# Graph network of two layers: four more groups of each layer from products, and another order at the border of two batches

## The chip, the core and the metric

The kernel runs on one core of a Trainium2 chip. The metric is the device time of one execution in microseconds. Before the change the median of three runs is 3701.22 us (3698.91 to 3702.09).

## What is computed

12,500 nodes carry 48 features, and 200,000 edges are sorted by their target `dst`. Cut to what matters, the reference is:

```
# layer 0
tmp = concatenate([x[dst], x[src], edge_attr_32], axis=1)
msg = relu(tmp @ W1 + b1) @ W2 + b2
x1  = layernorm(x + segment_sum(msg, dst))
# layer 1
m   = relu(x1[src] + edge_attr_48)
out = layernorm(x1 + (1 + eps) * x1 + segment_sum(m, dst))
```

For an edge's message, the row `x[src]` has to be fetched from an arbitrary place in the table. The sums over `dst` are local, since the edges are sorted.

## The kernel before

**Groups and steps.** The edges are cut into 391 groups of 512 (four tiles of 128 edges). Each layer is one loop over steps `k` (`run`, L620): in each step every stage runs for its own group, as in `(sum1, 1)`, which handles group `k - 1`. Nothing reorders the instructions: each engine's queue holds them in the order in which the Python code makes them, and a wait holds up everything behind it on that engine.

**Two ways to the source rows.** Most groups fetch their 512 rows by four indirect gathers that POOL makes (`gather`, L246, shown as L247), six groups ahead (`AHEAD`), in layer 1 into a pool of twelve buffers (`xs_pool`, L165). The groups of `PE_GROUPS0` (layer 0: 65, 85, ..., 16 groups) and `PE_GROUPS` (layer 1: 20, 30, ..., 38 groups) need no gather: TensorE makes their rows as products of one-hot matrices with the whole table, which lies on chip in three bf16 pieces (`xp`, 98 blocks of 128 rows).

**A batch of products** (`products`, L530) makes two groups, that is eight tiles. `place` (L479) has DVE write eight one-hots of the row within a block (`which_e`, L485), and PE transposes them into a PSUM tile `which` (L490). In layer 1 ACT makes a copy of it in SBUF (L539). Then for each of the 98 blocks an engine selects those edges whose source lies in that block: DVE from `which` (L495), or ACT in two instructions from the copy (L500, L502). PE multiplies each selected one-hot with the block (`multiply`, L507; eight products a block) into three PSUM tiles `ps`. These are opened and closed by matmuls of zeros (`edge_of`, L515). At the end DVE adds the three pieces into `made` (`take`, L523). Blocks are multiplied one step after they were selected.

In layer 1 a batch takes 20 steps of five blocks (`BPS`), the third by ACT (`BY_ACT = 2`). Its PSUM tiles come from `banks = ("pm", "ph", "ph", "pm")` with two buffers to each name: `ps` takes two buffers of `ph` and one of `pm`, `which` the other of `pm`. In layer 0 a batch takes 40 steps with two and three blocks in turn (`BPS0`), all selected by DVE, with one buffer to each tile.

**Layer 1's own stages.** `fill1` (L693) makes the one-hots of targets on DVE (`hot`, L695), from a pool `late` of four buffers (L686), two steps ahead. `message1` (L702) adds rows and edge features on DVE (`m`, L705 for gathered rows, L709 for products), and ACT takes the relu (`msg`, L711). `sum1` (L717) sums the group by four f32 matmuls (L725, two records each), one step later. Twelve groups share a PSUM bank, opened and closed by zeros (L722, L730). `drain1` (L734) adds a closed bank to the table of sums, and where a segment of 896 nodes is complete, `finish1` (L456) transposes its sums (L394) and DVE and ACT normalize and store them. The stages stand in this order within a step:

```
[(fetch1, -AHEAD), (fill1, -2), (sum1, 1), (drain1, 4), (message1, 0), (some_products, -AHEAD)]
```

Between the layers `front` (L759) makes six groups' rows of the last segment by products while the gathers of the other segments already run.

**Layer 0** has its stages in L567 to L618: transposes of the assembled rows (`turn0`, L587), two matrix products (L598, L613), relu (L602), and the window sums on DVE (L387). In its last steps the finished segments are loaded again by SP and split into the three pieces (`lead0`, L640; `END0`).

Of the kernel before, what the change touches and what calls it, by code (L numbers as in the profile page):

```python
# [32 lines left out]
F32 = mybir.dt.float32  # L33
I32 = mybir.dt.int32
BF16 = mybir.dt.bfloat16
# [4 lines left out]
P = 128  # L40
Q = 128
N = 12500
E = 200000
D = 48
# [4 lines left out]
NT = -(-N // Q)  # L49
# [9 lines left out]
NSEG = NT // NB  # L59
# [4 lines left out]
AHEAD = 6  # L64
# [3 lines left out]
GB = 12  # L68
FRONT = 6
FIRST = 20  # L70
EVERY = 10
NPE = 38
BEGIN1 = 4
BATCH = 2
BPS = 5
BY_ACT = 2
PIECES = 3

FIRST0 = 65
EVERY0 = 20  # L80
NPE0 = 16
BPS0 = (2, 3)
SPLIT0 = 2
BEGIN0 = 20
END0 = 341

PE_GROUPS0 = [FIRST0 + EVERY0 * i for i in range(NPE0)]
PE_GROUPS = [FIRST + EVERY * i for i in range(NPE)]
assert FRONT % BATCH == 0 and NPE % BATCH == 0
assert PE_GROUPS[0] >= FRONT  # L90

assert PE_GROUPS[-1] < NCHUNK and PE_GROUPS0[-1] < NCHUNK
assert 2 * NT < BATCH * EVERY0 * sum(BPS0) and BEGIN0 > SPLIT0 + NSEG + 1
assert CHUNK * N % E == 0
assert NSEG * NB == NT
STEP = CHUNK * N // E
# [64 lines left out]
def windowed(ctx, tc, dram, flag, x, src, dst, e32, e48, w1, b1, w2, b2, eps, out):  # L161
# [15 lines left out]
    psum = layer0.enter_context(tc.tile_pool(name="psum0", bufs=1, space=bass.MemoryType.PSUM))  # L177
# [109 lines left out]
    for op, by, plus, to in (  # L287
# [3 lines left out]
        nc.vector.tensor_scalar(  # L291
            bits[:, FRONT : FRONT + NPE, :], src_g[:, FIRST : PE_GROUPS[-1] + 1 : EVERY, :],
            by, None, op0=op,
        )
        nc.vector.tensor_scalar(
            bits[:, FRONT + NPE :, :], src_g[:, FIRST0 : PE_GROUPS0[-1] + 1 : EVERY0, :],
            by, None, op0=op,
        )
        nc.vector.tensor_scalar(to, bits, plus, None, op0=ALU.add)
    begin.close()  # L300
    onehots = layer0.enter_context(tc.tile_pool(name="onehots0", bufs=2 * max(BPS0)))
    product = layer0.enter_context(tc.tile_pool(name="product0", bufs=1))
# [126 lines left out]
    def rows_of(table, s):  # L429
        return table[s * SN : (s + 1) * SN, :].rearrange("(t p) d -> p t d", p=Q)  # L430

    def split(t, s):
        for i in range(PIECES):
            piece = xp[:, s * NB : (s + 1) * NB, i, :]
            nc.scalar.activation(piece, t, AF.Copy)
            if i < PIECES - 1:
                rest = node.tile([Q, NB, D], F32, name="rest")
                nc.vector.tensor_tensor(rest, t, piece, op=ALU.subtract)
                t = rest

    def finish0(s):
# [6 lines left out]
        if s < NSEG - 1:  # L448
            nc.scalar.dma_start(rows_of(front_dram, s), x1)
        if last_group(s) >= END0:  # L450
            split(x1, s)
# [15 lines left out]
    def last_group(s):  # L467

        return max(g for g in range(NCHUNK) if low(g) < (s + 1) * SN)
# [7 lines left out]
    PER = 512 // (PIECES * D)  # L477

    def place(first, tiles, name, bufs):  # L479

        which = psum.tile([Q, tiles, P], BF16, name=name, bufs=bufs)
        which_e = product.tile([P, tiles, Q], BF16, name="which_e")
        for j in range(tiles):
            i = first + j // TPC
            nc.vector.tensor_scalar(  # L485
                which_e[:, j, :], iota_1, part[:, i, j % TPC : j % TPC + 1],
                block[:, i, j % TPC : j % TPC + 1], op0=ALU.is_equal, op1=ALU.mult,
            )
        for j in range(tiles):
            nc.tensor.transpose(which[:, j, :], which_e[:, j, :], ident16)  # L490
        return which

    def select(which, b):
        o = onehots.tile([Q, which.shape[1], P], BF16, name="o")
        nc.vector.tensor_scalar(o, which, float(b + 1), None, op0=ALU.is_equal)  # L495
        return o

    def select_by_act(copy, b):
        square = product.tile([Q, copy.shape[1], P], BF16, name="square")
        nc.scalar.activation(square, copy, AF.Square, bias=less[:, b : b + 1])  # L500
        o = onehots.tile([Q, copy.shape[1], P], BF16, name="o_act", bufs=2)
        nc.scalar.activation(o, square, AF.Relu, bias=1.0, scale=-1.0)  # L502
        return o

    def multiply(ps, o, b):
        for j in range(o.shape[1]):
            nc.tensor.matmul(  # L507
                ps[j // PER][:, j % PER, :], o[:, j, :], xp[:, b, :, :],
                start=False, stop=False, skip_group_check=True,
            )  # L510

    def edge_of(ps, start):
        for t in ps:
            n = t.shape[1] * PIECES * D
            nc.tensor.matmul(  # L515
                t.rearrange("p k c d -> p (k c d)"), zeros[:, :P], zeros[:, :n],
                start=start, stop=not start,
            )

    def take(ps, first, batch):  # L520
        xs = product.tile([P, batch * TPC, D], F32, name="made", bufs=FRONT // BATCH)
        for k, t in enumerate(ps):
            nc.vector.tensor_reduce(  # L523
                xs[:, k * PER : k * PER + t.shape[1], :], t.rearrange("p k c d -> p k d c"),
                AX.X, ALU.add,
            )
        for i in range(batch):
            made[ahead[first + i]] = xs[:, i * TPC : (i + 1) * TPC, :]

    def products(begin, count, batch, blocks, per_step, by_act, banks, bufs):  # L530


        tiles = batch * TPC
        for first in range(begin, begin + count, batch):
            which = place(first, tiles, banks[0], bufs)
            copy = None
            if by_act is not None:
                copy = product.tile([Q, tiles, P], BF16, name="copy", bufs=2)
                nc.scalar.activation(copy, which, AF.Copy)  # L539
            ps = [  # L540
                psum.tile([P, min(PER, tiles - k), PIECES, D], F32, name=banks[1 + k // PER],
                          bufs=bufs)
                for k in range(0, tiles, PER)
            ]
            edge_of(ps, True)
            last = []
            todo, step = list(blocks), 0
            while todo:
                n = per_step[step % len(per_step)]
                now = [  # L550
                    (b, select_by_act(copy, b) if i == by_act else select(which, b))
                    for i, b in enumerate(todo[:n])
                ]
                todo, step = todo[n:], step + 1
                for c, o in last:
                    multiply(ps, o, c)
                last = now
                yield
            for c, o in last:
                multiply(ps, o, c)  # L560
            edge_of(ps, False)
            take(ps, first, batch)


    cat, h, pt, ph, pa, hot = {}, {}, {}, {}, {}, {}
# [54 lines left out]
    def run(stages, adds, finish, lead):  # L620
# [13 lines left out]

    whole = {}
    work0 = products(
        FRONT + NPE, NPE0, BATCH, range(NT), BPS0, None, ("which", "sums0", "sums1", "sums2"), 1
    )

    def lead0(k):  # L640
# [10 lines left out]
        for s in range(NSEG):  # L651
# [3 lines left out]
            if k == SPLIT0 + s + 2:  # L655
                split(whole.pop(s), s)
            if last_group(s) < END0:
                if k == END0 + 2 * s + 1:
                    whole[s] = seg.tile([Q, NB, D], F32, name="whole", bufs=2)
                    nc.sync.dma_start(whole[s], rows_of(x1_dram, s))  # L660
                if k == END0 + 2 * s + 4:
                    split(whole.pop(s), s)
# [7 lines left out]
    def fetch1(g, table):  # L670
        cat[g] = xs_pool.tile([P, TPC, D], F32, name="xs")
        for j in range(TPC):
            gather(cat[g][:, j, :], table, g, j)
# [9 lines left out]


    layer0.close()
    late = ctx.enter_context(tc.tile_pool(name="late", bufs=4))  # L686
    psum = ctx.enter_context(tc.tile_pool(name="psum", bufs=1, space=bass.MemoryType.PSUM))
    onehots = ctx.enter_context(tc.tile_pool(name="onehots", bufs=8))
    product = ctx.enter_context(tc.tile_pool(name="product", bufs=1))
# [67 lines left out]
    banks = ("pm", "ph", "ph", "pm")  # L757

    def front():  # L759
# [18 lines left out]
            before = ps, first  # L778
        take(*before, BATCH)

    rest = products(FRONT, NPE, BATCH, range(NT), (BPS,), BY_ACT, banks, 2)

    def some_products(g):
        if g >= BEGIN1:
            next(rest, None)
# [3 lines left out]
    def lead1(k):  # L789
        for s in range(NSEG):  # L790
# [3 lines left out]
    front()  # L794
    run(
        [(lambda g: g >= FRONT and g not in PE_GROUPS and fetch1(g, x1_dram), -AHEAD), (fill1, -2),
         (sum1, 1), (drain1, 4), (message1, 0), (some_products, -AHEAD)],
        None, None, lead1,
    )

# [210 lines left out]
```

## Time and profile before

| | |
|---|---|
| median of three runs | 3701.22 us |
| the profiled execution | 3699.33 us |
| its span, first to last instruction | 3697.6 us |
| mean granted TensorE clock | 0.885 |
| busy PE, PEld | 91%, 80% |
| busy DVE, ACT, POOL | 73%, 37%, 75% |
| gathers on POOL, layer 0 | 1500, 953 ns each |
| gathers on POOL, layer 1 | 1388 and 24, 951 and 958 ns each |
| products of batches (weight loads of L507) | 21,336 |

PE is the matmul queue, PEld its weight loads[...]. A PE that is shown busy is not PE at its peak, because matmuls overlap and because the clock that is granted to it changes. So the share of busy time alone does not tell which engine sets the pace. Times in the timeline are microseconds from the start of the span. Layer 0 ends near 1915 us with its last segment, the products of `front` lie between 1922 and 1957 us, and layer 1 runs from there to the end.

### The profile page before, as it was taken

Reading aid. Unit: us, or ns where it says so; the run is one execution under the profiler, and the core shown is the slowest. Engines: PE = TensorE matmul, PEld = TensorE weight load, DVE = VectorE, ACT = ScalarE, POOL = GpSimd, SP = SyncE. Lnnn points to the kernel's source line nnn. Section 1 sums busy time; section 2 is a strip of 40 time slices with the busy share of each in tenths; the row PEclk is TensorE's granted clock in tenths of the full one; section 3 lists DMA queues with packets and bytes.
Section 4 is the critical chain, followed back from the end, with each engine's and each line's share of the span. In section 5 each row is a group of like instructions: output and inputs, shape, how many; then the busy total and the mean of one; then the engine's idle time right before and its main releaser. Section 6 shows DMA issues by size and latency. Waiting matters only on the chain. (4 is left out here: it accounts for less than half of the span.)

```text
span 3697.6 us, 87599 instructions
## 1 busy us (share of the span) xinstructions
PE 3348.4 (91%) x33806; PEld 2968.8 (80%) x33806; DVE 2683.3 (73%) x5415; ACT 1365.6 (37%) x2178; POOL 2774.8 (75%) x2923
## 2 busy tenths in 40 slices
PE   5888998998999899887889999999999999999996
PEld 4887988897888798886768887888888888888884
DVE  4765876676777686674438788788878888888883
ACT  2211211121112121113215555565556555655562
POOL 7777777777777777777776777777777777777776
PEclk8887988898989898897659999999999999999996
DMA  4222222122222212223211122122212221222121
GB/s 94 50 50 44 47 50 52 39 55 47 46 47 53 51 44 49 49 48 68 46 35 37 43 46 46 42 52 46 46 43 46 51 46 37 52 46 51 37 52 35
DMA packets 326421, 177.43 MB, mean 48 GB/s; under 512 B 144384, under 2 KB 325744, under 8 KB 326000
## 3 DMA queue, kind: packets, MB, share of 16 engines
q0 software_dynamic: 93184, 71.75, 11.3%
q1 hardware_dynamic: 203152, 88.86, 9.0%
q10 hardware_dynamic: 29664, 11.16, 1.1%
q8 instruction: 269, 4.41, 0.5%
q14 instruction: 152, 1.25, 0.1%
HBM read 156.51 MB, written 15.03 MB: 46 GB/s over the span
## 5 line engine op out<-in xcount | busy, mean ns | idle before, releaser
L247 POOL DMA_INDIRECT cat<-in_x_dram,src_i x1500 | 1429.2, 953 | 460.8 <-issue 310.3
L247 POOL DMA_INDIRECT xs<-x_dram,src_i x1388 | 1320.0, 951 | 435.9 <-issue 291.1
L507 PEld LDWEIGHTS <-o 128*128 128x128 bf16 x18296 | 1250.4, 102 | 99.4 <-DVE o L495 41.9
L495 DVE TENSOR_SCALAR o<-pm 128x1024 bf16<-128x1024 bf16 x1503 | 942.5, 686 | 62.2 <-ACT copy L539 27.1
L507 PE MATMUL ph<-xp,o 128*128 128x144 bf16 x8976 | 808.8, 231 | 0.0
L602 ACT ACTIVATE h<-ph 128x512 f32<-128x512 f32 x391 | 233.0, 596 | 1110.7 <-PE pa L613 1086.1
L598 PE MATMUL ph<-wcat,cat_t 128*128 128x128 f32 x3128 | 507.4, 313 | 106.4 <-ACT h L602 106.3
L598 PEld LDWEIGHTS ph<-wcat,cat_t 128*128 128x128 f32 x3128 | 448.0, 221 | 127.4 <-ACT h L602 120.8
L725 PE MATMUL pt<-hot,msg 128*48 128x128 f32 x3128 | 447.9, 290 | 56.5 <-ACT msg L711 56.5
L495 DVE TENSOR_SCALAR o<-which 128x1024 bf16<-128x1024 bf16 x784 | 495.3, 680 | 3.1 <-PE which L490 3.0
L507 PE MATMUL sums<-xp,o 128*128 128x144 bf16 x6272 | 488.6, 238 | 0.0
L725 PEld LDWEIGHTS pt<-hot,msg 128*48 128x48 f32 x3128 | 341.0, 129 | 141.4 <-ACT msg L711 63.8
L507 PE MATMUL pm<-xp,o 128*128 128x144 bf16 x2978 | 438.9, 230 | 0.0
L613 PE MATMUL pa<-cat,h 128*128 128x48 f32 x3128 | 431.6, 285 | 5.4 <-DVE pa L606 5.1
L613 PEld LDWEIGHTS pa<-cat,h 128*128 128x128 f32 x3128 | 429.2, 212 | 6.8 <-issue 4.7
L500 ACT ACTIVATE square<-copy,less 128x1024 bf16<-128x1024 bf16 x380 | 430.7, 1133 | 0.7
L502 ACT ACTIVATE o_act<-square 128x1024 bf16<-128x1024 bf16 x380 | 401.6, 1057 | 17.2 <-PE pm L507 5.8
L587 PE MATMUL pt<-ident,cat 128*128 128x128 f32 x1564 | 292.4, 302 | 82.5 <-DMA cat<-in_x_dram,src_i 79.3
L695 DVE TENSOR_TENSOR hot<-pa,rel 128x512 f32<-128x512 f32 x391 | 269.8, 690 | 97.6 <-PE pt L725 96.6
L591 DVE COPY cat_t<-pt 128x512 f32<-128x512 f32 x391 | 266.9, 683 | 72.3 <-PE pt L587 68.9
L711 ACT ACTIVATE msg<-m 128x192 f32<-128x192 f32 x391 | 141.5, 362 | 456.9 <-DVE m L705 408.4
L587 PEld LDWEIGHTS pt<-ident,cat 128*128 128x128 f32 x1564 | 214.7, 171 | 110.2 <-DMA cat<-in_x_dram,src_i 105.7
(118 smaller groups left out, 2412.1 us busy)
## 6 DMA issues: line engine op xcount, KB each, us to landing
e48c<-in_e_dram SPq DMA_DIRECT2D x78, 480.0 KB
e32c<-in_e_dram SPq DMA_DIRECT2D x78, 320.0 KB
cat<-in_x_dram,src_i POOLq DMA_INDIRECT x1500
xs<-x_dram,src_i POOLq DMA_INDIRECT x1388
wcat<-a SPq DMA_DIRECT2D x391, 24.0 KB
a<-a ACTq DMA_DIRECT2D x14, 256.0 KB
a<-a ACTq DMA_DIRECT2D x14, 192.0 KB
x_seg<-in_x_dram SPq DMA_DIRECT2D x14, 168.0 KB
```

Of the source, the lines that this page charges most:

```text
L247: nc.gpsimd.indirect_dma_start(out=t, out_offset=None, in_=table, in_offset=bass.IndirectOffsetOnAxis(ap=src_i[:, g * TPC + j : g * TPC + ...
L495: nc.vector.tensor_scalar(o, which, float(b + 1), None, op0=ALU.is_equal)
L500: nc.scalar.activation(square, copy, AF.Square, bias=less[:, b : b + 1])
L502: nc.scalar.activation(o, square, AF.Relu, bias=1.0, scale=-1.0)
L507: nc.tensor.matmul(ps[j // PER][:, j % PER, :], o[:, j, :], xp[:, b, :, :], start=False, stop=False, skip_group_check=True,)
L587: nc.tensor.transpose(pt[g][:, j, :], cat[g][:, j, :], ident[:P, :P])
L591: nc.vector.tensor_copy(h[g], pt.pop(g))
L598: nc.tensor.matmul(ph[g][:, j, :], t[:, j, :], wcats[g % NW], start=True, stop=True)
L602: nc.scalar.activation(h[g], ph.pop(g), AF.Relu)
L613: nc.tensor.matmul(pa[g][:, 0, :], t[:, j, :], hot[:, j, :], start=j == 0, stop=j == TPC - 1)
L695: nc.vector.tensor_tensor(o, numbers[:, None, :].to_broadcast([P, TPC, W1]), rel1[:, g, :, None].to_broadcast([P, TPC, W1]), op=ALU.is_equal,)
L725: nc.tensor.matmul(bank[k][:, i * STEP : i * STEP + W1], msg[:, j, :], o[:, j, :], start=False, stop=False, skip_group_check=True,)
```

## The change

The change has these parts:

- Layer 0 makes 20 groups by products instead of 16 (58, 75, ...), three blocks in each step, so 33 steps a batch. `END0` moves from 341 to 352.
- Layer 1 makes 42 groups instead of 38 (20, 29, ...), with five and six blocks in turn, so 18 steps a batch. Of five blocks ACT selects the third, of six the second and the fifth. `o_act` has four buffers instead of two. The batches begin two steps later (`BEGIN1`).
- The pool `late` has six buffers instead of four, for `hot` and for `msg`.
- `sum1` and `drain1` run one step later.
- In `products`, `take` of a batch no longer follows its closing zeros. It stands in the next batch's first step, behind that batch's `place`, `copy` and first selects. The next batch's `ps` tiles are allocated and opened only after it.

```
-EVERY = 10
-NPE = 38
-BEGIN1 = 4
+EVERY = 9
+NPE = 42
+BEGIN1 = 6
-BPS = 5
-BY_ACT = 2
+BPS = (5, 6)
+BY_ACT = ((2,), (1, 4))
-FIRST0 = 65
-EVERY0 = 20
-NPE0 = 16
-BPS0 = (2, 3)
+FIRST0 = 58
+EVERY0 = 17
+NPE0 = 20
+BPS0 = (3,)
-END0 = 341
+END0 = 352
...
-        o = onehots.tile([Q, copy.shape[1], P], BF16, name="o_act", bufs=2)
+        o = onehots.tile([Q, copy.shape[1], P], BF16, name="o_act", bufs=4)
...
         tiles = batch * TPC
+        before = None
         for first in range(begin, begin + count, batch):
             which = place(first, tiles, banks[0], bufs)
...
-            ps = [
-                psum.tile([P, min(PER, tiles - k), PIECES, D], F32, name=banks[1 + k // PER],
-                          bufs=bufs)
-                for k in range(0, tiles, PER)
-            ]
-            edge_of(ps, True)
-            last = []
+            ps = last = None
             todo, step = list(blocks), 0
             while todo:
                 n = per_step[step % len(per_step)]
+                acts = by_act[step % len(by_act)] if by_act else ()
                 now = [
-                    (b, select_by_act(copy, b) if i == by_act else select(which, b))
+                    (b, select_by_act(copy, b) if i in acts else select(which, b))
                     for i, b in enumerate(todo[:n])
                 ]
                 todo, step = todo[n:], step + 1
-                for c, o in last:
-                    multiply(ps, o, c)
+                if ps is None:
+                    if before:
+                        take(*before)
+                    ps = [
+                        psum.tile([P, min(PER, tiles - k), PIECES, D], F32,
+                                  name=banks[1 + k // PER], bufs=bufs)
+                        for k in range(0, tiles, PER)
+                    ]
+                    edge_of(ps, True)
+                else:
+                    for c, o in last:
+                        multiply(ps, o, c)
                 last = now
                 yield
             for c, o in last:
                 multiply(ps, o, c)
             edge_of(ps, False)
-            take(ps, first, batch)
+            before = ps, first, batch
+        take(*before)
...
-    late = ctx.enter_context(tc.tile_pool(name="late", bufs=4))
+    late = ctx.enter_context(tc.tile_pool(name="late", bufs=6))
...
-         (sum1, 1), (drain1, 4), (message1, 0), (some_products, -AHEAD)],
+         (sum1, 2), (drain1, 5), (message1, 0), (some_products, -AHEAD)],
```

## What I expect

> **What bounds the kernel now.** I read the stretches of each layer first, then the waits, then the timeline of layer 1 at two places. Stretches (us, busy time and count of PE, PEld, DVE, ACT and POOL, granted clock, DMA share, GB/s), layer 0 and then layer 1:
>
> ```profile
> 150.00:1890.00 1740.00, 1537.92 (x14220) 1445.11 (x14218) 1172.71 (x2481) 334.42 (x831) 1317.61 (x1386) 0.86 0.23 49
> 1960.00:3680.00 1720.00, 1647.23 (x18601) 1385.24 (x18599) 1384.76 (x2635) 982.15 (x1232) 1297.27 (x1364) 0.93 0.21 46
> ```
>
> POOL starts a gather every 1.25 us in both layers (1740/1386, 1720/1364; 0.95 us each plus a 0.30 us gap). Gathers set the pace. But who waits for whom says how close the others are (waits of POOL after 1990 us, then of DVE in the whole run):
>
> ```profile
> POOL xs L247 <- DVE m L705: 9.1, 30, 0.3
> DVE m L705 <- DMA xs<-x_dram,src_i: 34.2, 12, 4.8
> ```
>
> POOL never really waits for a free buffer in layer 1, and DVE waits for gathered rows only 12 times, all after 3300 us. In the timeline a message's add starts 33 us after its gathers at group 17, 21 at group 173, 1.5 at group 389. So PE and DVE are just 32 us in 1,690 quicker than POOL: two bounds within 2%.
>
> What PE can do at most is read from a plain step, five blocks of products:
>
> ```profile
> 2673.03 1.07 PE L725 MATMUL pt<-hot,msg 128*48 128x128 f32 x8
> 2674.04 0.55 PE L507 MATMUL ph<-xp,o 128*128 128x144 bf16 x6
> 2674.55 0.54 PE L507 MATMUL ph<-xp,o 128*128 128x144 bf16 x6
> 2676.64 1.07 PE L725 MATMUL pt<-hot,msg 128*48 128x128 f32 x8
> ```
>
> A block of eight products takes 0.50 us, a step 3.61: 1.11 + 0.50 a block. Twenty of these are 72 us, but batches start every 88.3 us (first which_e at 1957, last at 3546, 18 intervals). The rest goes at the border of two batches:
>
> ```profile
> 2658.07 1.71 PE L515 MATMUL ph<-zeros 1*128 1x432 f32 x4
> 2659.09 1.33 DVE L523 TENSOR_REDUCE made<-ph 128x144 f32<-128x432 f32 x2 [5.18 <-PE ph L515]
> 2660.71 2.15 DVE L485 TENSOR_SCALAR which_e<-iota,part,block 128x128 bf16<-128x128 f32 x8
> 2661.12 2.08 PE L490 MATMUL pm<-ident,which_e 128*128 128x128 bf16 x8 [0.85 <-DVE which_e L485]
> 2663.13 3.24 PE L515 MATMUL ph<-zeros 1*128 1x432 f32 x4
> 2663.24 1.02 ACT L539 ACTIVATE copy<-pm 128x1024 bf16<-128x1024 bf16 x1 [8.93 <-PE pm L490]
> 2664.30 2.48 DVE L495 TENSOR_SCALAR o<-pm 128x1024 bf16<-128x1024 bf16 x4 [1.44 <-ACT copy L539]
> 2667.27 1.94 PE L725 MATMUL pt<-hot,msg 128*48 128x128 f32 x8
> 2669.14 0.90 PE L507 MATMUL ph<-xp,o 128*128 128x144 bf16 x6
> ```
>
> and in the stretches around it, where the last three columns are clock, DMA and GB/s:
>
> ```profile
> 2658.10:2661.60 3.50, 2.62 (x9) 1.19 (x8) 2.39 (x7) 0.00 (x0) 2.59 (x4) 1.00 0.09 17
> 2661.60:2665.00 3.40, 3.37 (x9) 1.72 (x10) 1.96 (x7) 1.73 (x2) 2.55 (x3) 0.50 0.14 22
> 2668.50:2671.90 3.40, 3.40 (x28) 3.03 (x27) 3.40 (x7) 2.71 (x4) 2.48 (x4) 0.51 0.55 161
> ```
>
> After a thin stretch PE's clock is halved for some 10 us, at every border; the opening zeros and the sum (1.07 → 1.94) take double.
>
> **Gathers removed.** Four more groups in each layer are made by products: 16 gathers each. On POOL alone that is 2 x 16 x 1.25 = 40 us. In layer 0 POOL keeps the bound, I think: its pace falls from 4.79 to 371 x 4 x 1.25 / 391 = 4.74 us a step, and a full-clock PE step with three blocks, which becomes the rule, takes 3.72 us (1335.04 to 1338.76; 3.22 with two). One microsecond a step is spare for borders (ten, not eight) and for the segment ends, after which layer 0 catches up today. Without that cover two batches would cost about 2 x 55 us of PE. I take the full 20 us; between 0 and 20 it can be. END0 moves the reloads (SP) and splits (ACT, DVE) of twelve segments eleven steps later. SP's wcat loads queue behind these reloads as they do now (SP waited 25.7 us in ten times at L660), and no products run there in either kernel: nothing.
>
> **Layer 1: PE's work of a batch at full clock.** Before, 20 steps: 98 x 0.50 + 20 x 1.11 = 71.2; opening and closing zeros 2 x 2.1; eight transposes 0.5; the zeros of layer 1's banks, 1.86 us in twelve steps, 3.1; segment ends' transposes 0.4. Sum 79.4, so 8.9 of 88.3 are lost. After, 18 steps of five and six blocks: 49 + 20 = 69.0, + 4.2 + 0.5 + 2.8 + 0.4 = 76.9. POOL then wants only 16 groups x 4 x 1.25 = 80.0 for 18 steps (88.3 stands against 90 today). So PE may lose 3.1 us a batch, where it loses 8.9 now.
>
> **The border after.** Today I count: 11.1 us from closing zeros to products with 5.7 of work, so 5.4 lost, and 2.7 us of products at half clock, 1.35: 6.8. Segment ends (PE waits 2.77 us for msg at 2615.86, mostly followed by one slow window) make 4.0 x 14/19 = 2.9. That is 9.7 against 8.9 measured, so I scale by 0.92.
>
> The new order takes DVE's 5.18 us wait away: which_e is made while PE still multiplies, and the transposes run unpaced (0.5). But take now stands behind the first part's selects, and the new opening zeros need the banks that take reads (ph has two buffers, both in one batch). PE has nothing else in its queue: the next sum and products stand behind these zeros. So PE idles: copy 1.02, which the first select waits for, four selects 2.48, first reduce 0.61, hand-overs 0.25: 4.35 us. Before, that chain ran beside the opening zeros. The thin stretch is longer than today's, so the clock is halved again: zeros 2.1 and sum 1.0 at double time, 3.1, and 1.35 of products. 8.8 x 0.92 = 8.1.
>
> **Sums a step later, six one-hots.** No cost in work. The sum behind a segment end no longer needs the newest message, but the products still need selects that DVE makes after some 4.4 us of normalization (2610.52 to 2615.06), against 4.1 us of PE work ahead: of 4.0 I leave 2.0 (0.7 to 4). 2.0 x 14/21 = 1.3. DVE's waits for hot (96.6 us) go, but they only showed that DVE was ahead of PE.
>
> **Blocks to ACT.** A batch has 27 on ACT instead of 20, 71 on DVE instead of 78. ACT: 27 x 2.23 + 18 x 0.3 + 2 = 68 us; DVE 71 x 0.63 + 18 x 1.05 + 8 = 72: both below PE, so nothing.
>
> **Sum.** Period 76.9 + 8.1 + 1.3 = 86.3, times 21. First batch: 1957 − 20 + 2 (BEGIN1) = 1939. The last twelve messages then have their rows: 12 x 1.05 of DVE, and 16 us from the last add to the end (3681 to 3697.6), about 32. 1939 + 21 x 86.3 + 32 = 3783 of span; with 1.7 us around it (3699.33 against 3697.6) and 1.9 to the median, 3787 us, 2.3% slower. POOL will be stopped by full buffers.
>
> **Two rules against the rows.** The Trainium skill, "TensorE: Matmul & The Clock Gate", "Part 1: The HAM clock gate", wants about one idle window of 3.4 us before the clock falls. Here gaps of 1 us and paced work sufficed, at each of 19 borders. By the rule a 4.35 us gap holds a whole window in 28% of cases (0.95/3.4), so half-clock work costs 0.28 x 4.4 = 1.2, and segment ends 1.0: 76.9 + 4.35 + 1.2 + 1.0 = 83.5, 3728 us. I take the row. The same page's "Back-to-back issue gap" gives 81 ns per weight load and matmul at 128 columns, which speaks harder against added products: 784 x 0.081 = 63.5 instead of 49, 4091 us. The row shows 62.5 ns at 144 columns and decides.
>
> **Rivals.**
> A. POOL stays the bound: 3699 − 40 + 2 = 3661. It holds if a period stays under 80, and the change is faster below 82. For it: three waits really go. Against it: 76.9 of work and 4.35 of idle time that no other instruction fills. 7%.
> B. PE bounds, but being denser it keeps its clock: 76.9 + 4.35 + 0.7 (segment ends' wait alone) = 82.0, 3696 us. Against it: the stretches above. 13%, lying around no change.
> C. ACT sets the six-block steps: 2 x 2.23 + 0.3 = 4.76 against 4.11, if four o_act buffers do not even out the pairs (7.29 against 7.72): 9 x 0.65 more a batch, 3910. 6%.
> The forecast has 74%, its own range 3745 to 3830 (84.3 to 88.3 a batch).
>
> Faster by over 0.2% (about what a measurement can tell): A and part of B, 0.12; within, 0.05; slower 0.83. The range 3696 to 3840 leaves out A, the lower part of B, and C.
>
> **What would show it.** Border: an idle PE of about 4.4 us before L515, ended by made L523; clock 0.5 for two or three windows after each; batches every 86 us. POOL waiting for m for over 50 us in layer 1, and no longer DVE for xs. Layer 1 starting about 20 us earlier. I am wrong if the opening zeros do not wait for take, if the clock stays at 1.0 across borders, or if batches come every 80 us with POOL unbroken.

## The result and the profile after

The changed kernel takes 3860.24 us (median of 4 runs, 3857.5 to 3863.9), beside 3700.44 us before: ratio 1.0434 (95% interval 1.0417 to 1.045). The profiled execution has a span of 3855.7 us, 158.1 more than before and 72.7 more than the predicted 3783. Some experiments below fell on chips on which every kernel took about half as long again (the kernel before 5471 to 5548 us), with many short gaps of PE for which the profile shows no cause; they are called starved below, and their ratios are not set beside those of the others.

First the stretches of the two layers after the change (columns as in the prediction):

```profile
150.00:1870.00 1720.00, 1571.17 (x15749) 1502.77 (x15746) 1282.52 (x2685) 332.09 (x829) 1280.70 (x1351) 0.89 0.22 49
1960.00:3840.00 1880.00, 1758.47 (x20208) 1491.60 (x20207) 1416.57 (x2679) 1376.81 (x1608) 1277.93 (x1348) 0.91 0.19 42
```

In layer 1 POOL starts a gather every 1.39 us (1880/1348) and no longer every 1.25 to 1.26. It is not the bound any more. PE is, at a lower clock than before (0.91 against 0.93). The waits of the changed kernel name what stops them (us in total, times, longest):

```profile
POOL xs L247 <- DVE m L713: 193.7, 59, 12.5
...
PE ph L515 <- DVE made L523: 84.8, 20, 4.2
...
POOL cat L247 <- ACT h L610: 34.7, 31, 6.3
...
PE sums L515 <- DVE made L523: 23.3, 9, 2.6
```

and of the kernel before:

```profile
POOL xs L247 <- DVE m L705: 22.3, 31, 13.2
...
POOL cat L247 <- ACT h L602: 10.1, 33, 0.3
```

The first row is POOL in layer 1 stopped by full buffers, which was 22.3 us before. The second is new: at each of 20 borders of two batches, PE waits 4.24 us until the first reduce of `take` has read its bank. The third is POOL in layer 0, stopped too: before, none of these waits was longer than 0.3 us. The fourth is the new wait for `take` in layer 0, at nine borders of its ten batches, 2.6 us each. One border in the timeline of the changed kernel (here and below, rows in between are left out):

```profile
2579.49 1.71 PE L515 MATMUL ph<-zeros 1*128 1x432 f32 x4
2581.62 0.62 PE L490 MATMUL pm<-ident,which_e 128*128 128x128 bf16 x8
2582.28 1.02 ACT L541 ACTIVATE copy<-pm 128x1024 bf16<-128x1024 bf16 x1 [3.19 <-PE pm L490]
2583.34 2.48 DVE L495 TENSOR_SCALAR o<-pm 128x1024 bf16<-128x1024 bf16 x4 [4.58 <-ACT copy L541]
2585.74 1.11 DVE L523 TENSOR_REDUCE made<-ph 128x144 f32<-128x432 f32 x2
2586.48 3.21 PE L515 MATMUL ph<-zeros 1*128 1x432 f32 x4 [4.24 <-DVE made L523]
2590.58 1.94 PE L733 MATMUL pt<-hot,msg 128*48 128x128 f32 x8
2592.46 0.90 PE L507 MATMUL ph<-xp,o 128*128 128x144 bf16 x6
2596.09 0.54 PE L507 MATMUL ph<-xp,o 128*128 128x144 bf16 x6
```

Read it downwards as a chain: transposes end, ACT copies, DVE selects four blocks, only then the first reduce reads the bank, and only then PE opens the next batch. What follows runs at twice its time (zeros 3.21, sum 1.94, products 0.90 where 1.71, 1.07 and 0.54 is full speed), until 2595.9. The stretches around it show when the clock fell:

```profile
2579.00:2582.40 3.40, 3.24 (x22) 1.86 (x20) 0.00 (x0) 0.21 (x2) 2.49 (x4) 0.97 0.12 20
2582.40:2585.80 3.40, 0.00 (x0) 0.00 (x0) 2.46 (x5) 3.11 (x3) 2.79 (x3) 0.50 0.13 22
2585.80:2589.20 3.40, 2.72 (x4) 1.48 (x5) 3.40 (x9) 1.09 (x2) 0.86 (x2) 0.50 0.04 7
...
2592.60:2596.00 3.40, 3.40 (x31) 3.40 (x30) 1.38 (x2) 2.62 (x4) 0.42 (x1) 0.52 0.06 10
2596.00:2599.40 3.40, 3.40 (x48) 3.10 (x46) 2.80 (x5) 0.93 (x2) 0.69 (x1) 1.00 0.02 5
```

The clock is already 0.50 while PE waits, which costs nothing by itself, and stays there for over nine more microseconds in which PE works.

To compare kernels I split the time between the first `which_e` of a batch and of the next: PE's idle gaps; half of the time in which PE worked while the granted clock was 0.5 (an estimate of what it lost by that); and the rest, which is its work at full clock. Means per batch of layer 1, the end of layer 0's last gather, and the first batch's `which_e`, which I take as the start of layer 1 (all in us):

| kernel (label of its run) | period | work | idle | clock loss | last gather of layer 0 | first batch |
|---|---|---|---|---|---|---|
| before | 88.3 | 80.0 | 2.7 | 5.6 | 1893.2 | 1956.6 |
| after | 88.1 | 76.5 | 5.6 | 6.0 | 1896.4 | 1964.6 |
| take_mid3 | 83.2 | 76.6 | 1.6 | 5.0 | 1868.2 | 1936.7 |
| fill4 | 85.1 | 80.0 | 1.7 | 3.3 | 1897.4 | 1969.8 |
| take_old3 | 85.5 | 77.5 | 2.6 | 5.4 | 1892.5 | 1960.7 |
| mid38b | 87.9 | 79.8 | 2.9 | 5.2 | 1869.1 | 1939.7 |

### The profile page after: what moved, and what is told of

Its sections match the earlier page's. It is cut to its first block, busy times and chain, and to the rows that moved or that the text cites. A ratio compares the mean times of both kernels' runs of the same rounds, so it can differ in the third digit from the quotient of the medians.

```text
span 3855.7 us, 94680 instructions
## 1 busy us (share of the span) xinstructions
PE 3512.2 (91%) x37022; PEld 3150.9 (82%) x37022; DVE 2827.9 (73%) x5664; ACT 1760.3 (46%) x2558; POOL 2735.8 (71%) x2891
## 4 chain that ended last, share of the span: by engine, by line
PE 78%; DVE 6%; DMA 5%; issue 4%; ACT 3%; POOL 3%; ACTq 0%; DVEq 0%; SPq 0%; POOLq 0%
PE ph L507 19%; PE sums L507 12%; PE ph L606 9%; PE pt L733 9%; PE pa L621 8%; PE pm L507 6%; PE pt L595 4%; PE ph L515 3%; DMA cat<-in_x_dram,src_i 3%; POOL cat L247 2%; DVE o L495 2%; PE sums L515 2%; DMA xs<-x_dram,src_i 1%; POOL xs L247 1%; PE px L329 1%
## 5 line engine op out<-in xcount | busy, mean ns | idle before, releaser
L247 POOL DMA_INDIRECT cat<-in_x_dram,src_i x1484 | 1409.6, 950 | 483.6 <-issue 307.3
L507 PEld LDWEIGHTS <-o 128*128 128x128 bf16 x19936 | 1362.0, 101 | 126.9 <-DVE o L495 62.7
L495 DVE TENSOR_SCALAR o<-pm 128x1024 bf16<-128x1024 bf16 x1512 | 976.4, 686 | 405.4 <-PE pm L507 232.7
L495 DVE TENSOR_SCALAR o<-which 128x1024 bf16<-128x1024 bf16 x980 | 614.3, 680 | 54.0 <-PE which L490 49.0
L500 ACT ACTIVATE square<-copy,less 128x1024 bf16<-128x1024 bf16 x567 | 645.5, 1138 | 6.9
L502 ACT ACTIVATE o_act<-square 128x1024 bf16<-128x1024 bf16 x567 | 599.2, 1057 | 19.4 <-PE pm L507 1.4
L507 PE MATMUL sums<-xp,o 128*128 128x144 bf16 x7840 | 585.7, 236 | 0.0
L507 PEld LDWEIGHTS <-o_act 128*128 128x128 bf16 x4536 | 312.8, 100 | 21.2 <-ACT o_act L502 21.2
L507 PE MATMUL ph<-xp,o_act 128*128 128x144 bf16 x3402 | 315.4, 231 | 15.0 <-ACT o_act L502 15.0
L595 PE MATMUL pt<-ident,cat 128*128 128x128 f32 x1564 | 272.0, 298 | 19.0 <-DMA cat<-in_x_dram,src_i 16.0
```

Of the source, the lines that this page charges most:

```text
L247: nc.gpsimd.indirect_dma_start(out=t, out_offset=None, in_=table, in_offset=bass.IndirectOffsetOnAxis(ap=src_i[:, g * TPC + j : g * TPC + ...
L507: nc.tensor.matmul(ps[j // PER][:, j % PER, :], o[:, j, :], xp[:, b, :, :], start=False, stop=False, skip_group_check=True,)
L595: nc.tensor.transpose(pt[g][:, j, :], cat[g][:, j, :], ident[:P, :P])
```

## The experiments

Two theories. "Border": the new place of `take` makes PE wait at every border, keeps its clock low, and leaves layer 0 no room to catch up. "Load": PE has more products to do, and where `take` stands does not matter.

**The sum's read between the first copies and ACT's copy** (all else as changed, both layers; three runs of one kernel):

```
             which = place(first, tiles, banks[0], bufs)
+            if before:
+                take(*before)
             copy = None
...
                 if ps is None:
-                    if before:
-                        take(*before)
                     ps = [
```

> The changed kernel with take between place and the copy: which_e is still made early, but take runs while PE transposes and ACT copies, and stands ahead of the first selects. Theory border: PE waits under 1 us for the opening zeros instead of 4.24, and the clock is low for a shorter time: 88.1 falls to about 83 us a batch, 3860 - 21 x 5 = 3755 us. Theory load: not below 3830 us.

> The changed kernel with take between place and the copy, once more, since in the first runs [...]the kernel before took 5473 us. Theory border: PE waits under 1 us for the opening zeros instead of 4.24, the clock is low for a shorter time, about 83 us a batch: 3755 us. Theory load, PE's added work is the loss: not below 3830 us.

> The changed kernel with take between place and the copy, a third time[...]. Theory border: PE waits under 1 us for the opening zeros instead of 4.24 and about 83 us a batch: 3755 us. Theory load: not below 3830 us. If the kernel before takes some 5500 us again, [...]the ratio of the two says little about the border: 1.00 to 1.01 as in the two runs before.

take_mid and take_mid2 fell on starved chips: 5495.83 and 5491.78 us, ratios 1.004 (1.0019 to 1.0061) and 1.0036 (1.002 to 1.0053). take_mid3 took 3728.78 us beside 3700.86, ratio 1.008 (1.006 to 1.0099): 131 us less than the changed kernel, for moving three reductions a few instructions forward. Its border in the timeline:

```profile
2518.42 1.71 PE L515 MATMUL ph<-zeros 1*128 1x432 f32 x4
2519.45 1.33 DVE L523 TENSOR_REDUCE made<-ph 128x144 f32<-128x432 f32 x2 [1.76 <-PE ph L515]
2520.66 1.03 PE L490 MATMUL pm<-ident,which_e 128*128 128x128 bf16 x8
2521.62 3.25 PE L515 MATMUL ph<-zeros 1*128 1x432 f32 x4
2525.76 1.94 PE L733 MATMUL pt<-hot,msg 128*48 128x128 f32 x8
```

The reduce now runs beside the transposes, and the opening zeros follow without a gap. The table shows where the time goes: 4.0 us of idle time and 1.0 of clock loss a batch, 4.9 x 21 = 103, and layer 1 starts 28 us earlier. Its work per batch is that of the changed kernel. So 131 of the 160 us hang on where `take` stands, and "load" as stated is refuted. The clock falls at this border too, though PE does not wait behind the closing zeros.

**PE kept busy while it waits** (64 matmuls of the identity by itself, into a bank that is not read, at layer 1's borders):

```
             which = place(first, tiles, banks[0], bufs)
+            if by_act is not None and before:
+                fill = psum.tile([P, P], F32, name="px")
+                for _ in range(64):
+                    nc.tensor.matmul(fill, ident16, ident16, start=True, stop=True)
             copy = None
```

> The changed kernel with 64 idle bf16 matmuls of 128 columns behind the transposes at each border of layer 1, into a PSUM tile that nobody reads; they take up PE's 4.24 us wait and add no time to it. Theory clock: half of the border's loss is the halved clock that follows the wait; with the wait filled the clock stays up, and a batch loses some 4 us less: 3860 - 21 x 4 = 3775 us. Rival, the wait alone is the loss, or the clock falls anyway: 3855 to 3870 us.

> The changed kernel with 64 idle bf16 matmuls behind the transposes at each border of layer 1, once more[...]. Theory clock: the wait filled, the clock stays up at the borders, and a batch loses some 4 us less: 3860 - 21 x 4 = 3775 us. Rival, the wait alone is the loss, or the clock falls anyway: 3855 to 3870 us.

> The changed kernel with 64 idle bf16 matmuls of 128 columns behind the transposes at each border of layer 1; they take up PE's 4.24 us wait and add no time to it. Theory clock: half of the border's loss is the halved clock that follows the wait; filled, a batch loses some 4 us less: 3860 - 21 x 4 = 3775 us. Rival, the wait alone is the loss, or the clock falls anyway: 3855 to 3870 us.

> The changed kernel with 64 small matmuls of the identity by itself behind the transposes of every batch of layer 1, into a bank that is not read, so that PE does not idle while it waits for the sum's read: the wait stays, and only the clock can change. If the halved clock behind the border is most of its loss, zeros and products behind it run at full speed, less than 5 us a batch at half clock instead of 15, period 84 or less, 3775 us, against 3860 for the change. If the wait alone is the loss, or the clock falls for another reason, 3855 to 3870 (ratio 1.042 to 1.046). Where PE is short of instructions, ratio 1.016 as before.

fill, fill2 and fill3 fell on starved chips: 5558.41, 5641.47 and 5624.69 us, ratios 1.0156 (1.0123 to 1.0189), 1.0158 (1.0109 to 1.0208) and 1.0161 (1.0123 to 1.0199). fill4 took 3801.11 us, ratio 1.0259 (1.0234 to 1.0284): 59 us less than the changed kernel, with 64 more matmuls a batch. Neither number expected was met (3775; 3855 to 3870). The border of fill4, and the stretches around it:

```profile
2568.97 5.06 PE L541 MATMUL px<-ident 128*128 128x128 bf16 x64
2572.67 1.11 DVE L523 TENSOR_REDUCE made<-ph 128x144 f32<-128x432 f32 x2
2573.95 1.71 PE L515 MATMUL ph<-zeros 1*128 1x432 f32 x4
2576.08 1.07 PE L737 MATMUL pt<-hot,msg 128*48 128x128 f32 x8
2577.09 0.55 PE L507 MATMUL ph<-xp,o 128*128 128x144 bf16 x6
...
2566.00:2569.40 3.40, 3.40 (x22) 2.23 (x20) 0.00 (x0) 0.19 (x1) 2.49 (x4) 0.84 0.14 16
2569.40:2572.80 3.40, 3.40 (x44) 3.40 (x42) 2.54 (x5) 3.04 (x3) 2.38 (x3) 0.66 0.14 20
2572.80:2576.20 3.40, 3.40 (x29) 2.20 (x27) 3.40 (x8) 1.16 (x2) 0.93 (x1) 1.00 0.09 12
```

The wait is still there in substance (PE does nothing useful for 5 us). The clock still falls, at 2568.3, but it is back after 3.4 us, while the filler runs, and so zeros, sum and products behind it run at full speed. Clock loss falls by 2.7 us a batch, 56 in 21 batches; the filler takes 3.5 us, slightly less than the 3.9 us of idle time that it replaces, and layer 0 is as before the edit. So about 56 us of the border's cost are halved clock that can be bought back without touching the wait. The idle time that take_mid3 removed was 4.0 x 21 = 84 us; no run did both.

**The sum's read back in its old place** (all else as changed, both layers):

```
-            before = ps, first, batch
-        take(*before)
+            take(ps, first, batch)
```

> The changed kernel, with take directly behind the closing zeros again, in both layers. Theory border: the place of take costs PE 4.24 us of waiting per batch of layer 1 and a longer time at half clock; back at the old place a border loses about 7 us instead of 9.5, so 21 x 2.5 = 53 us less, and layer 0 gets some 10 us back: 3795 us. Theory load: the loss is PE's added work, the order at the border matters little: 3845 to 3860 us. If the new place helps in spite of all: over 3870 us.

> The changed kernel with take directly behind the closing zeros again, in both layers; take between place and the copy gave 3729 us. Theory border: the old place makes DVE wait for the closing zeros ahead of which_e and paces the transposes, a border of 7 us as before: about 85.5 us a batch, 3800 us, between the changed kernel and the one with take in the middle. Theory load with a lucky middle: over 3845 us.

> The changed kernel with the sum's read directly behind its batch's closing zeros in both layers, as in the kernel before; all else as changed. Border theory: no wait of 4.2 us for the read, but which_e is late again at each border (5 us, of which PE loses what it lost in the kernel before, 6.8 to 8.9 with the segment ends): 74.7 + 9 = 84 to 85.5 a batch, and layer 0 without stalls of POOL, 3760 us (3740 to 3800). Load theory: the place of the read does not matter, 3850 to 3870. Where PE is short of instructions, ratio 1.017 as before.

take_old and take_old2 fell on starved chips: 5566.95 and 5636.97 us, ratios 1.0168 (1.0127 to 1.0209) and 1.0192 (1.0156 to 1.0229). take_old3 took 3787.12 us, ratio 1.0221 (1.0204 to 1.0238). So the move of `take` lost 73 us, and everything else in the change together lost 84 (against the kernel before on the same chip, 3702.65). That rest is "load" in this sense: with 42 groups PE bounds layer 1 at 85.5 us a batch, where POOL would want 80.0 by its pace of 1.25 us a gather. The old place is also not the best one: at take_mid3's, behind the writes of `which_e` and ahead of the selects, the kernel is over 50 us faster. In layer 0 POOL is stopped here too: 11 gaps of over 0.35 us make 26.4 us, against 12 and 31.4 in the changed kernel and none in take_mid3 (the start left out). The old place is no cure there.

**Layer 1's changes alone** (the new `take` in layer 1; layer 0 with its 16 groups and old `take`):

```
-FIRST0 = 58
-EVERY0 = 17
-NPE0 = 20
-BPS0 = (3,)
+FIRST0 = 65
+EVERY0 = 20
+NPE0 = 16
+BPS0 = (2, 3)
...
-            before = ps, first, batch
-        take(*before)
+            if behind:
+                before = ps, first, batch
+            else:
+                take(ps, first, batch)
+        if before:
+            take(*before)
```

> Layer 1 as changed (42 groups, take behind the selects there), layer 0 as before (16 groups, take at the old place there). Layer 1 now begins at 1965 us in the changed kernel and at 1957 before, of which 2.5 us are BEGIN1. Theory: layer 0's part is worth nothing either way, its 20 us of gathers are lost to full buffers: 3853 us. Rival, layer 0's part still brings a gain that is hidden behind something later: 3870 us or more.

> Layer 1 as changed (42 groups, take behind the selects there), layer 0 as before (16 groups, take at the old place there). Layer 1 begins at 1965 us in the changed kernel and at 1957 before, of which 2.5 us are BEGIN1. Theory: layer 0's part is worth nothing either way, its 20 us of gathers are lost to full buffers: 3853 us. Rival, layer 0's part brings a gain that shows only later: 3870 us or more.

Both fell on starved chips: 5583.21 and 5669.01 us, ratios 1.0206 (1.0174 to 1.0238) and 1.0248 (1.0211 to 1.0285). They do not answer what layer 1's part alone costs on a chip like that of the prediction, and no other run does. The changed kernel itself was not run on a starved chip, so they cannot be set beside it either.

**The moved read with the old load in layer 1** (layer 0 with 20 groups, six buffers, sums a step later, the read between the first copies and ACT's copy; added to the first edit of this section):

```
-EVERY = 9
-NPE = 42
-BEGIN1 = 6
+EVERY = 10
+NPE = 38
+BEGIN1 = 4
...
-BPS = (5, 6)
-BY_ACT = ((2,), (1, 4))
+BPS = (5,)
+BY_ACT = ((2,),)
```

> The change's layer 0 (20 groups), six buffers and later sums, but layer 1's load of before (38 groups, every tenth, five blocks a step), and the sum's read put between the first copies and ACT's copy. Border theory: PE's work of a batch falls under the 88 to 90 us that POOL wants, since the border loses 2 us and not 9, so POOL's gathers set the pace in both layers again; layer 1 starts 20 us earlier than in the kernel before: 3675 us (ratio 0.993). Load theory: the added products of layer 0 and the later sums cost PE what they take from POOL: 3700 or more, ratio at or above 1.

> The change's layer 0 (20 groups), six buffers and later sums, layer 1's load of before (38 groups, every tenth, five blocks a step), the sum's read between the first copies and ACT's copy, in both layers. Border theory: PE loses about 7 us a batch and needs 79.9 + 7 = 87, under the 88.3 to 90 that POOL needs, so POOL's gathers set the pace in both layers; layer 1 starts 20 us earlier than in the kernel before: 3675 us (ratio 0.993). Load theory: what layer 0 saves on POOL is lost on PE in layer 1: 3695 to 3705.

mid38 fell on a starved chip: 5412.67 us, ratio 0.9894 (0.9831 to 0.9957). mid38b took 3675.04 us, ratio 0.9919 (0.9902 to 0.9935): faster than both kernels, at the 3675 us that "border" gave. One row of its waits shows which engine sets the pace:

```profile
DVE m L713 <- DMA xs<-x_dram,src_i: 188.1, 101, 4.6
```

DVE now waits 101 times for gathered rows, 12 times before: PE and DVE run ahead of POOL. Layer 0's last gather ends 24 us earlier than before (1869.1 against 1893.2), and POOL's gaps there are 2 with 2.6 us instead of the changed kernel's 12 with 31.4. So the gain that was found lies in layer 0, and it came only with the borders short.

## Why the prediction was wrong

The sign and the mechanism in layer 1 were right; the time lay 20 us above the range. Two terms of the sum failed: what layer 0 gains, in its mechanism, and the halved clock behind layer 1's border, in its size. The 72.7 us of span that were missing, term by term:

- **Start of layer 1, predicted 1939, measured 1964.6: 25.6 us.** The step that failed is "I take the full 20 us" of layer 0, from "one microsecond a step is spare for borders and for the segment ends". Layer 0's last gather came 3.2 us later than before, not 20 earlier. POOL stopped for 31.4 us in 12 gaps, the longest (6.26 us, at 1169) some 20 us after a segment end's work on PE; the kernel before has no such gap. I had put layer 0's borders inside the spare microsecond, without a term for `take`, for which PE waited 23.3 us there. That wait is not the whole reason: take_old3 is without it, and POOL is stopped all the same. The reserve had been 1.3 us a step (4.79 − 3.47, with two and three blocks in turn) and became 1.0 (4.74 − 3.72); that this is why PE no longer catches up in time is argued, not shown. What is shown is that the two runs with the read in between got 24 to 25 us. My own lower end for this term, 0, would have been the better choice, and the true value lay outside even that. The other 2.4 us lie between the last gather and the first batch.
- **Period, predicted 86.3, measured 88.13: 1.83 x 21 = 38.4 us.** PE's work of a batch was right: 76.9 predicted, 76.5 measured. The wait was right as well: 4.35 against 4.24 us, ended by `made` as foreseen, and 4.0 of idle time on average in batches without a segment end. The mis-sized term is the clock after it. I let zeros, sum and 2.7 us of products run at half speed, 4.45 us lost. In batches without a segment end PE worked 11.4 us at half clock, so it lost 5.7; of the 20 spells at borders ten last 13.7 us and three 23.9, one of them from 2667.6. With my factor of 0.92, which came from today's border and had no reason to hold for another, the border was put at 8.1 instead of 4.0 + 5.7 = 9.7. Segment ends cost 1.9 us a batch (idle 2.65, clock 0.5, in 12 of 20 batches), not 1.3. Together 1.6 + 0.6 − 0.4 = 1.8.
- **Tail, predicted 32, measured 40.4 by this count: 8.4 us** (3855.7 − 1964.6 − 21 x 88.13). This is no cost of its own, but the mark that I count batches by. At the last border of the changed kernel `which_e` begins 6.5 us ahead of the closing zeros, where in take_old3, as in the kernel before, it begins 2.6 behind them. So the last batch, counted from its `which_e`, holds a border more, and the first one, which has none, is short:

```profile
3727.29 2.14 DVE L485 TENSOR_SCALAR which_e<-iota,part,block 128x128 bf16<-128x128 f32 x8
3733.79 1.71 PE L515 MATMUL ph<-zeros 1*128 1x432 f32 x4
...
3825.51 1.71 PE L515 MATMUL ph<-zeros 1*128 1x432 f32 x4
```

From the last closing zeros to the end it takes 30.2 us in the changed kernel and also in take_old3: the tail of 32 was right. Counted to these zeros, the first batch takes 79.0 us and the 20 others 89.1 each, 1861 us where I had 21 x 86.3 = 1812. So the batches are 48 us off, not 38.

Point by point otherwise: POOL was stopped by full buffers in layer 1 as said (193.7 us, over 50). ACT's blocks cost little (PE waited 15.0 us in all for `o_act`), so rival C did not happen. Rival A, the period under 80 with POOL unbroken, fell on PE's side altogether: even with the short border of take_mid3 a batch takes 83.2 us. Rival B needed PE to keep its clock; it fell at every border, and fill4 got it back sooner, but by 64 matmuls more.

The rule that I set against the row (the Trainium skill, "TensorE: Matmul & The Clock Gate", "Part 1: The HAM clock gate") would have given 3728 us for the wait as it is. The row was right to be taken: in take_mid3 the clock falls without any idle window. My reading of it was still too mild: clock loss at a border was 5.7 us a batch, where I had 4.45 (before my factor) and that rule 1.2. What the sums a step later and the six buffers bring was not tried by itself; mid38b contains them and is faster than the kernel before.

## What to carry to other kernels

When a step is put behind other work to hide a wait, ask which engine owns the buffers that it frees: here PE could not open the next batch until a reduce, queued on DVE behind four selects, had read the last one. Put such a read behind what its engine can do before the data are there (`which_e`), and ahead of what has to wait for something else (the selects): 3729 us, against 3787 ahead of both and 3860 behind both. And before relieving the bounding engine, work out the time that the next one needs with its borders. The two were within 2% of each other here: 20 us of relief in layer 0 were worth nothing until the borders were cut, and four groups more in layer 1 cost 54 us even with short borders (take_mid3 against mid38b).

## What the runs showed of the hardware

TensorE's clock can halve without any gap. At 19 of the 20 borders of layer 1 in take_mid3, the profile shows no idle moment of PE in the 3.4 us before the granted clock falls. The border shown above is the other one: the last gap of PE is 0.6 us long and ends at 2517.8, and the clock falls at 2520.4, at the end of the closing zeros (from 2518.42). Transposes, opening zeros and sum then take double (the opening zeros 3.25 us instead of 1.71). In fill4 the clock falls at every border too, but at 16 of 20 it is back after 3.4 us, while the 64 full matmuls run; in the changed kernel the low spells at borders last 10.2 to 23.9 us. That zeros with one row of weights count as little activity fits both, but was not measured by itself.

On the starved chips every kernel ran about 1.5 times as long. One row of the waits of take_old's run there (`issue` is time in which the engine waited for nothing that the profile shows):

```profile
PEld L507 <- issue: 797.9, 1211, 2.0
```

The same row holds 26.2 us in the kernel before and 33.7 in the changed one on the other chips. The texts on record call this a lack of instructions; that is a reading, and what starves PE there was not found. Of the four kernels that shared one such chip the one with the moved read is still the fastest (take_mid 1.004, fill 1.0156, take_old 1.0168, l1_only 1.0206), but filling PE's wait brings nothing measurable against take_old, where on the other chips the old place of the read is 14 us ahead of the filler.
